# Attention on one core: the value products of a set of scores, issued two sets later and between the halves of a set

## The chip, the core and the metric

The kernel runs on one core of a Trainium2 chip. Its time is the device time of one execution, in microseconds (us); the number to beat or miss is the median of three runs of the kernel before, 2207.93 us (2204.1 to 2208.98). A profile of one execution stands beside it: it was taken in an execution of its own, and that execution has its own time.

The core has engines that run their own instruction streams in order and meet through semaphores: TensorE (PE, with its weight loads shown apart as PEld), VectorE (DVE), ScalarE (ACT), GpSimd (POOL), and SyncE (SP), which issues most of the DMAs.

## The reference, cut to what matters

The block is an attention layer, a mixture of experts, a small mixing layer and the same mixture of experts again, each added to its input. Only the attention is touched. There are 2 sequences of 2048 tokens with 256 features, 16 heads of 16 features, a causal mask, and everything is in float32:

```python
qkv = sn_dense(batch, W_qkv, u_qkv, sigma_qkv)          # x @ (sigma_param / sigma * W)
q, k, v = split_heads(q), split_heads(k), split_heads(v)
att = jnp.einsum('bhqd,bhkd->bhqk', q, k) * scale
att = jnp.where(causal[None, None] == 0, big_neg, att)
att = jax.nn.softmax(att, axis=-1)
x = jnp.einsum('bhqk,bhkd->bhqd', att, v)
x = sn_dense(x, W_proj, u_proj, sigma_proj)
```

## The kernel before

**Tiling.** A *unit* is one sequence b, one chunk c of 512 queries and one group g of 4 heads: 2 x 4 x 4 = 32 units. Each unit has as many *sets* as there are blocks of 128 keys up to its chunk: 4, 8, 12 or 16, 320 in all. The last 4 blocks of keys lie on the diagonal, where a set works on 512, 384, 256 and 128 columns; all other sets have 512. A unit takes its diagonal sets first (`softmaxes`).

**Two passes over the scores.** The row maxima must be known before the exponentials. So the scores are computed twice: once to find the maxima (`Maxima.step`, tiles `psm`, line 341; VectorE reduces each tile, lines 350 and 355), and once more transposed, with the maximum folded in through an extra row of q (`softmaxes`, tiles `st`, line 386; ScalarE takes the exponential into `pt`, line 390; GpSimd blanks the part above the diagonal, line 393). The maxima run some units ahead of the exponentials, and one loop walks both: in one turn of the loop it issues one set of the one and one set of the other.

**One turn of the loop.** A set has two halves of two heads each. In each half come two score products (`st`) and then two products for the maxima (`psm`) on the other half of the array's rows. These products use 32 rows each, so four of them run side by side. Behind the two halves come the *value products* of the set before (`values`, tile `o`, line 405): four products of 128 rows and 32 columns. ScalarE copies `o` out (line 414, or 411 for the first set of a unit), and GpSimd adds it to the accumulator `oa` (line 416). The variable `behind` holds the one set whose value products are still to come.

**What else goes into a turn.** Behind the value products come, in turns that are fixed by a plan: the projection to q and k of a later unit (`prepare`: two transposes `flip`, line 129, then `psk`, line 275, which ScalarE copies out twice, to `qT` and `sk`, lines 285 and 287), the values of a chunk (`make_v`, `psv`, line 301), the end of a unit (`finish`, `pso`, line 423, which VectorE reads, lines 426 and 429), and the output projection of a chunk (`project`: `psf`, line 444, copied by ScalarE; `psj`, line 454, read by VectorE). `after(k, ...)` puts such work at the end of a later turn; this text calls it *side work*.

**What sets the order.** Program order is the order of each engine. All accumulators named above except `st` come from one pool of 4 banks (`ps_m`, function `bank`), handed out round robin: a product may only start when the tile that had its bank four requests earlier has been read out. `st` has two tiles of its own (`ps_st`), `pt` six buffers.

Of the kernel before, what the change touches and what calls it, by code (L numbers as in the profile page):

```python
# [51 lines left out]
def hybrid_block(  # L52
# [87 lines left out]
    with tc.tile_pool(name="aw", bufs=1) as aw, ExitStack() as aw_ctx:  # L140
# [106 lines left out]
        with ExitStack() as ac:  # L247
# [16 lines left out]
            def bank(nm):  # L264
                return ps_m.tile([P, CH], F32, tag="mm", name=nm)
# [135 lines left out]
            def values(b, c, g, n, kb, off, pts):  # L401

                o = bank(f"o_{b}_{g}_{c}_{kb}")
                for j in range(4):
                    nc.tensor.matmul(  # L405
                        o[32 * j:32 * j + 32, off:], V[kb // NB][:, kb % NB, 4 * g + j, :],
                        pts[j // 2][:, j % 2, off:], start=True, stop=True,
                    )
                if n == 0:
                    acc[b, c, g] = oap.tile([P, CH], F32, tag="oa", name=f"oa_{b}_{g}_{c}")  # L410
                    nc.scalar.copy(acc[b, c, g], o)
                else:
                    t = oap.tile([P, CH], F32, tag="op", name=f"op_{b}_{g}_{c}_{kb}", bufs=2)
                    nc.scalar.copy(t[:, off:], o[:, off:])  # L414
                    a = acc[b, c, g]
                    nc.gpsimd.tensor_tensor(a[:, off:], a[:, off:], t[:, off:], ALU.add)  # L416
# [80 lines left out]
            def make_vs(b, c):  # L497

                todo = [(b, c, 0), (b, c, 2)] if (b, c) != LAST else []
                if b == LAST[0] and c == order[b][0]:  # L500
                    todo += [(*LAST, 0), (*LAST, 2)]
                for k, v in enumerate(todo):
                    after(k + 1, make_v, *v)

            tick = [0]
            due = []
# [1 line left out]
            def after(k, fn, *args):  # L508
                due.append((tick[0] + k, fn, args))
# [8 lines left out]
            def count(c):  # L518
                return NB * (c + 1)

            ready, mx, sm, behind = {}, None, None, None
            nm, na = 0, 0
            def scaled(f):
                factors["k"] = f
# [21 lines left out]
            while na < len(units) or due or behind:  # L546
                cols, n_m = CH, CH
                run_a = na < len(units) and ready.get(na, tick[0] + 1) <= tick[0]
                run_m = nm < len(units) and nm - na < QTS - 1 - (nm < EARLY)
                if run_a:  # L550
                    u = units[na]
                    if sm is None:
                        sm = softmaxes(*u)
                        left_a = count(u[1])
                        if u[2] == 0 and u[0] == 1:
                            make_vs(u[0], u[1])
                    done = count(u[1]) - left_a
                    cols = CH - done * P if done < NB else CH
                if run_m:
                    w = units[nm]  # L560
                    if mx is None:
# [4 lines left out]
                        mx = Maxima(*w)  # L566
# [6 lines left out]
                    kc, i = mx.pick(cols)  # L573
                    n_m = (i + 1) * P if kc == w[1] else CH
                for h in range(2):
                    if run_a:
                        got = next(sm)
                    if run_m:
                        mx.step(kc, i, 2 - 2 * h)
                if behind:  # L580
                    values(*behind)
                    behind = None
                if run_a:
                    behind = (*u, *got)
                    left_a -= 1
                    if not left_a:
                        sm, na = None, na + 1
                        after(4, finish, *u)
                        if u[2] == NG - 1:
                            box = {}  # L590
                            for k, i in enumerate((0, 2, 0, 2)):
                                after(5 + k, project, u[0], u[1], i, box)
                if run_m:
                    small_set = n_m <= 256 or not run_a
                    if steps and (small_set or steps == 3 or mx.left <= steps + 1):
# [8 lines left out]
                    if not mx.left:  # L604
                        shift(*w, mx.part, nmax[nm % 2])
                        ready[nm] = tick[0] + LAG
                        mx, nm = None, nm + 1
# [702 lines left out]
```

## Time and profile before

| | |
|---|---|
| median of 3 runs | 2207.93 us (2204.1 to 2208.98) |
| the profiled execution, its own time | 2117.58 us |
| its span, first to last instruction | 2115.8 us |
| mean granted TensorE clock in it | 0.983 |
| attention: first maxima products to last value products | 27.6 to 1139.7 us |
| PE busy over the span | 2010.0 us (95%) |
| DVE busy | 1386.0 us (66%) |
| ACT busy | 1075.5 us (51%) |
| POOL busy | 870.5 us (41%) |

The attention takes a little over half of the span; the experts and the mixing layer follow. "PE busy" counts a stretch in which any product is under way as busy, so gaps of part of the array don't show in it. The start times of the products in the timeline tell more than the share. In the trace each float32 product is two instructions, which are called its two passes in this text: the 4 value products of a set are 8 rows, the 8 products of its two halves are 16.

### The profile page before, as it was taken

Reading aid. Unit: us, or ns where it says so; the run is one execution under the profiler, and the core shown is the slowest. Engines: PE = TensorE matmul, PEld = TensorE weight load, DVE = VectorE, ACT = ScalarE, POOL = GpSimd, SP = SyncE. Lnnn points to the kernel's source line nnn. Section 1 sums busy time; section 2 is a strip of 40 time slices with the busy share of each in tenths; the row PEclk is TensorE's granted clock in tenths of the full one; section 3 lists DMA queues with packets and bytes.
Section 4 is the critical chain, followed back from the end, with each engine's and each line's share of the span. In section 5 each row is a group of like instructions: output and inputs, shape, how many; then the busy total and the mean of one; then the engine's idle time right before and its main releaser. Section 6 shows DMA issues by size and latency. Waiting matters only on the chain.

```text
span 2115.8 us, 36162 instructions
## 1 busy us (share of the span) xinstructions
PE 2010.0 (95%) x11840; PEld 1087.9 (51%) x11840; DVE 1386.0 (66%) x3428; ACT 1075.5 (51%) x1566; POOL 870.5 (41%) x1153
## 2 busy tenths in 40 slices
PE   6999999999999999999998999999999999999993
PEld 3444444444445444444444666655656556655662
DVE  4777777787776777777851546446776378663643
ACT  1657577577776667767784122324433244431330
POOL 4334345254343343434454171605422753346305
PEclk8999999999999999999999999999999999999997
DMA  3212110000000000000002321423210332013523
GB/s 97 77 36 64 34 33 5 10 1 7 6 7 6 6 1 7 4 4 4 2 2 86 135 90 46 150 80 113 80 41 18 130 112 78 28 40 134 165 76 121
DMA packets 87604, 113.04 MB, mean 53 GB/s; under 512 B 16385, under 2 KB 75137, under 8 KB 87297
## 3 DMA queue, kind: packets, MB, share of 16 engines
q1 hardware_dynamic: 73488, 75.08, 11.1%
q0 software_dynamic: 12288, 33.57, 4.8%
q8 instruction: 101, 1.65, 0.3%
q10 hardware_dynamic: 1648, 2.10, 0.3%
q14 instruction: 79, 0.64, 0.1%
HBM read 54.59 MB, written 51.64 MB: 50 GB/s over the span
## 4 chain that ended last, share of the span: by engine, by line
PE 82%; DVE 7%; ACT 3%; issue 3%; POOL 3%; DMA 2%; DVEq 0%; SPq 0%; POOLq 0%; ACTq 0%
PE st L386 15%; PE o L405 13%; PE psm L341 13%; PE eu L1085 10%; PE s L1011 7%; PE ed L1109 5%; PE sy L1028 4%; PE psk L275 3%; PE tr L1070 3%; PE psz L961 1%; PE psj L454 1%; POOL xs L893 1%; PE psv L301 1%; DVE junk L350 1%; PE psl L761 1%
## 5 line engine op out<-in xcount | busy, mean ns | idle before, releaser
L390 ACT ACTIVATE pt<-st 128x1024 f32<-128x1024 f32 (+3 forms) x640 | 556.0, 895 | 176.1 <-PE psm L341 123.3
L341 PE MATMUL psm<-kT,qT 32*128 32x512 f32 (+3 forms) x2560 | 621.8, 565 | 10.7 <-DMA kT<-sk 4.4
L386 PE MATMUL st<-qT,kT 32*128 32x512 f32 (+3 forms) x2560 | 604.8, 553 | 1.3 <-ACT pt L390 1.3
L355 DVE TENSOR_REDUCE part<-psm 128x1 f32<-128x512 f32 x768 | 477.1, 681 | 117.1 <-PE psm L341 113.6
L416 POOL TENSOR_TENSOR oa<-oa,op 128x512 f32<-128x512 f32 (+3 forms) x288 | 313.8, 1090 | 450.5 <-ACT op L414 450.0
L386 PEld LDWEIGHTS st<-qT,kT 32*128 32x128 f32 x2560 | 264.4, 184 | 228.0 <-ACT pt L390 140.5
L341 PEld LDWEIGHTS psm<-kT,qT 32*128 32x128 f32 x2560 | 274.6, 184 | 76.0 <-issue 20.1
L350 DVE CUSTOM_DVE_ANT_0 junk<-psm,maskq 128x384 bf16<-128x384 f32 (+3 forms) x512 | 250.8, 490 | 94.8 <-PE psm L341 29.9
L405 PE MATMUL o<-pt,v 128*32 128x512 f32 (+3 forms) x2560 | 301.2, 541 | 11.2 <-DVE part L355 6.7
L1085 PE MATMUL eu<-we,turned 128*128 x560 | 263.7, 593 | 0.0
L1092 ACT ACTIVATE es<-ea 128x256 f32<-128x256 f32 x156 | 65.0, 417 | 353.9 <-DVE ea L1090 353.8
L1011 PE MATMUL s<-xT_f,ws 128*128 128x512 f32 x512 | 232.6, 598 | 0.0
L920 POOL DMA_INDIRECT yg<-ys,slot x128 | 128.2, 1001 | 233.2 <-issue 84.6
L414 ACT COPY op<-o 128x512 f32<-128x512 f32 (+3 forms) x288 | 148.6, 516 | 64.5 <-PE o L405 46.9
L1090 DVE TENSOR_TENSOR ea<-eu,be 128x512 f32<-128x512 f32 x156 | 107.4, 689 | 109.5 <-PE eu L1085 108.9
L1109 PE MATMUL ed<-we,turned 128*128 x624 | 162.7, 383 | 14.5 <-ACT turned L1075 14.5
L393 POOL TENSOR_SCALAR_AFFINE_SELECT pt<-pt 128x256 f32<-128x256 f32 x256 | 103.0, 409 | 176.9 <-ACT pt L390 173.0
L405 PEld LDWEIGHTS o<-pt,v 128*32 128x32 f32 x2560 | 52.2, 108 | 214.4 <-DVE part L355 124.4
L1109 PEld LDWEIGHTS ed<-we,turned 128*128 128x128 f32 x624 | 116.1, 190 | 88.0 <-issue 49.0
L893 POOL DMA_INDIRECT xs<-xn_f,slot x128 | 124.9, 975 | 86.3 <-DVE slot L847 59.3
L1011 PEld LDWEIGHTS s<-xT_f,ws 128*128 128x128 f32 x512 | 95.3, 192 | 102.7 <-issue 96.4
L1085 PEld LDWEIGHTS eu<-we,turned 128*128 128x128 f32 x560 | 97.6, 190 | 75.1 <-issue 72.9
(268 smaller groups left out, 2099.4 us busy)
## 6 DMA issues: line engine op xcount, KB each, us to landing
xs<-xs SPq DMA_DIRECT2D x156, 128.0 KB
ys<-ey SPq DMA_DIRECT2D x156, 128.0 KB
xs<-zeros SPq DMA_DIRECT2D x78, 128.0 KB
we<-in_we_dram SPq DMA_DIRECT2D x8, 768.0 KB
kT<-sk SPq DMA_DIRECT2D x128, 32.0 KB
out_dram<-x SPq DMA_DIRECT2D x8, 512.0 KB
x<-in_x_dram SPq DMA_DIRECT2D x6, 512.0 KB
be<-in_be_dram SPq DMA_DIRECT2D x1, 3072.0 KB
```

The lines of the kernel that those rows point to most:

```text
L341: nc.tensor.matmul(ps[:, :n], self.q[r, i * P:(i + 1) * P], kT[b, g, kc][r, :n], start=True, stop=True,)
L350: nc.vector.tensor_tensor_reduce(junk[:, :n], ps[:, :n], maskq[:, CH - n:], 1.0, LOW, ALU.add, ALU.max, m,)
L355: nc.vector.reduce_max(m, ps[:, :n], axis=AX.X)
L386: nc.tensor.matmul(st[:, i, off:], k[r, ks], q[r, off:], start=True, stop=True)
L390: nc.scalar.activation(pt[:, :, off:], st[:, :, off:], AF.Exp)
L405: nc.tensor.matmul(o[32 * j:32 * j + 32, off:], V[kb // NB][:, kb % NB, 4 * g + j, :], pts[j // 2][:, j % 2, off:], start=True, stop=True,)
L414: nc.scalar.copy(t[:, off:], o[:, off:])
L416: nc.gpsimd.tensor_tensor(a[:, off:], a[:, off:], t[:, off:], ALU.add)
L893: ins = nc.gpsimd.indirect_dma_start(out=XS[b], out_offset=bass.IndirectOffsetOnAxis(ap=slots[f, b][:, k, n:n + 1], axis=0), in_=xhat[f, b ...
L1011: nc.tensor.matmul(ps, w[:, d, cs], xT[:, d, :], start=d == 0, stop=d == 1)
L1085: nc.tensor.matmul(ps, t[:, 1, d * P:(d + 1) * P], we_s[:, bass.ds(v + d * CH, CH)], start=d == 0, stop=d == 1,)
L1109: nc.tensor.matmul(ps[:, 0:D], t[:, 0, d * P:(d + 1) * P], we_s[:, bass.ds(v + 2 * CH + d * D, D)], start=d == 0, stop=d == 1,)
```

## The change

The value products of a set are issued two turns later instead of one, and between the first and the second half of that turn instead of behind both. For this `behind` becomes a list. When no score set is left to issue, one entry per turn is taken all the same. The end of a unit, the output projection and the values of the second sequence move back by one turn with it. Nothing else changes: no product, copy or DMA is added or removed.

```diff
@@ make_vs
-                    after(k + 1, make_v, *v)
+                    after(k + 2, make_v, *v)
@@
-            ready, mx, sm, behind = {}, None, None, None
+            ready, mx, sm, behind = {}, None, None, []
@@ one turn of the loop
                 for h in range(2):
                     if run_a:
                         got = next(sm)
                     if run_m:
                         mx.step(kc, i, 2 - 2 * h)
-                if behind:
-                    values(*behind)
-                    behind = None
+                    if not h and len(behind) > run_a:
+
+                        values(*behind.pop(0))
                 if run_a:
-                    behind = (*u, *got)
+                    behind.append((*u, *got))
                     left_a -= 1
                     if not left_a:
                         sm, na = None, na + 1
-                        after(4, finish, *u)
+                        after(5, finish, *u)
                         if u[2] == NG - 1:
                             box = {}
                             for k, i in enumerate((0, 2, 0, 2)):
-                                after(5 + k, project, u[0], u[1], i, box)
+                                after(6 + k, project, u[0], u[1], i, box)
```

## The prediction, made before the changed kernel was run

> **What bounds the kernel now.** I read the page first (busy shares, then the chain that ended last), then the waits of the weight loads inside the attention, then the timeline of PE over a few turns. From the page:
>
> ```profile
> PE 2010.0 (95%) x11840; PEld 1087.9 (51%) x11840; DVE 1386.0 (66%) x3428; ACT 1075.5 (51%) x1566; POOL 870.5 (41%) x1153
> PE 82%; DVE 7%; ACT 3%; issue 3%; POOL 3%; DMA 2%; DVEq 0%; SPq 0%; POOLq 0%; ACTq 0%
> PE st L386 15%; PE o L405 13%; PE psm L341 13%; PE eu L1085 10%; PE s L1011 7%; PE ed L1109 5%; PE sy L1028 4%; PE psk L275 3%; PE tr L1070 3%; PE psz L961 1%; PE psj L454 1%; POOL xs L893 1%; PE psv L301 1%; DVE junk L350 1%; PE psl L761 1%
> ```
>
> TensorE carries 82% of the chain, and the three kinds of product of the attention are 41% of it. So time is won or lost by what lies between PE's products. The timeline of PE over one plain turn (start, duration, engine, line, operation, tile, shape, count):
>
> ```profile
> 536.60 0.70 PE L386 MATMUL st<-qT,kT 32*128 32x512 f32 x2
> 537.13 0.59 PE L386 MATMUL st<-qT,kT 32*128 32x512 f32 x2
> 537.57 0.59 PE L386 MATMUL st<-qT,kT 32*128 32x512 f32 x2
> 538.00 0.59 PE L386 MATMUL st<-qT,kT 32*128 32x512 f32 x2
> 538.56 1.06 PE L405 MATMUL o<-pt,v 128*32 128x512 f32 x8
> 539.55 0.70 PE L386 MATMUL st<-qT,kT 32*128 32x512 f32 x2
> ```
>
> Look at the differences of the starts. Inside the scores a pass costs 0.43 us. The first pass behind another kind of product costs 0.53, and from the last pass to the value products it is 0.56. The value products take 0.99 until the scores go on. So a turn is 1.96 + 0.99 = 2.95 us, of which 1.96 - 4 x 0.43 = 0.24 us is the price of entering and leaving the 32-row products. The next turn takes 3.10 (538.56 to the value products at 541.66): every other turn one `psm` is 0.15 to 0.19 late, because VectorE has not yet read its bank. VectorE needs 2.4 us per turn (4 reductions 0.60 apart) and idles 0.5 to 0.8 between them. PE and VectorE are thus nearly in balance.
>
> A turn with side work is different:
>
> ```profile
> 550.68 1.06 PE L405 MATMUL o<-pt,v 128*32 128x512 f32 x8
> 551.68 1.98 PE L275 MATMUL psk<-xnTa,w_qkv 128*128 128x512 f32 x4
> 553.59 0.70 PE L386 MATMUL st<-qT,kT 32*128 32x512 f32 x2
> 555.02 1.12 PE L341 MATMUL psm<-kT,qT 32*128 32x512 f32 x2
> 556.07 1.06 PE L405 MATMUL o<-pt,v 128*32 128x512 f32 x8
> ```
>
> From `o` to `o` it is 5.39 us, though 2.95 + 1.91 (551.68 to 553.59) = 4.86 would do. The fourth `psm` starts at 555.02, where 554.56 was due. Its bank is that of `psk` (four requests earlier), and ScalarE reads that out only in these rows (the second ends at 554.97):
>
> ```profile
> 553.70 0.69 ACT L285 ACTIVATE qT<-psk,fq 128x512 f32<-128x512 f32 x1 [1.24 <-PE psk L275]
> 554.29 0.68 ACT L287 ACTIVATE sk<-psk,f_qkv 128x512 f32<-128x512 f32 x1
> ```
>
> The same on the diagonal, with 128 columns: the block of scores that starts at 582.75 needs 1.48 us to the value products at 584.23, because `psm` waits for `sk`:
>
> ```profile
> 582.22 0.60 PE L423 MATMUL pso<-ident,oa 128*128 128x128 f32 x4
> 583.74 0.56 PE L341 MATMUL psm<-kT,qT 32*128 32x128 f32 x4 [0.26 <-ACT sk L287]
> 584.23 0.64 PE L405 MATMUL o<-pt,v 128*32 128x256 f32 x8
> ```
>
> Last, what the weight loads waited for between 50 and 1142 us (total us, times, longest):
>
> ```profile
> PEld o L405 <- DVE part L355: 124.4, 154, 3.2
> PEld o L405 <- POOL oa L416: 14.9, 19, 0.9
> PEld psm L341 <- ACT sk L287: 12.1, 27, 1.1
> PEld o L405 <- POOL pt L393: 10.6, 17, 1.2
> PEld psm L341 <- DVE v L306: 5.9, 11, 0.9
> ```
>
> The large first row is mostly no loss: in the plain turn above the load of `o` sits 0.76 us idle while the products before it still stream.
>
> **The change, part by part.** *Plain turns: nothing.* Call the half behind the value products X and the other one Y. Before: o X Y o X Y. After: also o X Y o X Y, only that X is now the second half of one set and Y the first half of the next. The banks, ScalarE's order (exponential, exponential, copy of `o`) and VectorE's order turn with it. So the 2.95/3.10 alternation stays. The cover is complete: the same waits with other names.
>
> *Boundaries between kinds of product: a loss.* Side work stood behind the value products, where PE changed its kind anyway. Now it splits X from Y. I counted in the instruction order of both kernels: unbroken runs of 32-row products go from 335 to 423, runs of side work from 93 to 106, runs of value products stay near 319. A run of scores costs 0.24 extra at 512 columns (above); with 128 columns I take 0.20. A run of side work costs 1.91 - 4 x 0.43 = 0.19. So 88 x 0.22 + 13 x 0.19 = 22 us more on PE, if nothing hides it. Here a rule of the Trainium skill speaks against the change: "TensorEngine Tiling (Array Packing)", Tiling Modes, Key Properties, says that a change of the tiling mode, not of the tile alone, drains TensorE. The trace shows that the price exists and how large it is. By the rule alone the sum ends here: slower by 22. By the rows there is a second term, since the split also moves a wait.
>
> *Bank waits behind side work: a gain.* Before, the requests ran o, K, X1, X2, Y1, Y2: Y2 gets the bank of the side work K, one block of scores behind it. After, they run o, X1, X2, K, Y1, Y2, o, X1: the bank of K goes to the X1 behind the next value products, about 1 us (Y) + 1 us (o) later. ScalarE needs 1.4 us for `qT` and `sk`, so the wait is gone. For `psk` in a plain turn: 4.86 + 0.24 = 5.10 instead of 5.39, a gain of 0.29; about 10 such turns, -3 us.
>
> *The diagonal.* I walked one unit by hand with the rows' numbers (pass 0.43, 0.32, 0.22, 0.11; entering +0.10, leaving +0.1; VectorE per `psm` 0.60, and with the mask 0.71, 0.575, 0.44 for 384, 256, 128 columns; a product is readable 0.67 behind its last pass at 512). From the first diagonal set of the unit (572.23) to the seventh turn's scores (590.86) it takes 18.63 us before. After, with time from that same start: the 384 set starts at 2.94 (before 2.96), 256 at 5.85 (5.67), then `psk` alone at 8.56, 128 at 10.47 (10.52), where the second half waits 0.2 for `sk`, `pso` at 12.3, the next sets at 12.9 and 15.5, then a wait for VectorE of about 0.5, and the point with equal work done at 18.1 to 18.2. So -0.45 per unit, with the extra boundaries already in it. VectorE's idle time shrinks by as much, because X1 and X2 give it something to read while K runs (before it sat 2.39 us idle beside `psk`). This holds for units whose diagonal turns carry `psk`, `pso` or `flip`: 24 of 32, -11 us. My walk is good to some 0.3 us per unit, so 24 x 0.3 = 7 us either way.
>
> *Side work that had no such wait.* `psf`, `psj`, lone `flip` and `psv`: some 54 runs. They are small, or are read out quickly, and lose up to 0.24 each with nothing in return, 13 us at most; on the diagonal VectorE is late anyway and hides about half. I take +6.
>
> *GpSimd.* `o` waited for `pt` behind GpSimd's blanking and its 1.27 us addition (14.9 + 10.6 us of load waits). With two sets of lag they are done long before. Most of these waits lay under running products; comparing starts on PE I find 4 us that delayed products. -4 us. The addition moves between the two blankings on GpSimd's queue, which delays the second by 1.3 us; nothing needs it for another set.
>
> *What else moves.* SP's queue keeps its order (the same `kT` and `qT` DMAs in the same turns). `finish`, `project` and `make_v` go one turn later; they are due by the order of the queue, not by time. `pt` has six buffers for three sets: the exponential of set t reuses the buffer of set t-3, whose value products are issued a turn earlier, so no wait. Only the slack of a whole turn becomes half a turn. Last turns: one drained entry more, below 1 us. I value these at nothing, and at 0 to 5 us lost if the six buffers do bind.
>
> The sum: -3 - 11 + 6 - 4 = -12, from about -25 to +15. I round the likeliest to -10, since the walk left out every wait that I didn't see in the trace. The sum is made against the profiled execution, 2117.6 us; the median is 2207.9, 4% longer, and the trace doesn't show what those runs spend it on. I take the same -10 off the median: 2198. Two tenths of a per cent, about 4.4 us, is what can be told from no change.
>
> **The rivals.** *The boundaries decide.* If the waits behind side work only stood in for VectorE's lateness, they come back at the next bank and the split is paid in full: 22 us minus the 4 of GpSimd, +18 us, 2226. It speaks for it that VectorE is late on each diagonal (0.7 us more than the products need even in turns of 256 columns without side work); against it, that VectorE idles 1.66 and 2.39 us next to side work. The point is 0.22 us: where a turn with side work gets back less than that, the change loses. *The two terms cancel*: the diagonal yields 0.2 us per unit instead of 0.45, the rest stays: -3 - 5 + 8 - 2 = -2, 2206. *It is a rotation and more*: VectorE's shorter idle stretches also end the alternation 2.95/3.10 in the plain turns. There are about 176 of them, 0.075 each, -13 on top of -12: 2183. Against it: by the bank order the same late reduction meets the same kind of product.
>
> **How the numbers follow.** The likeliest case (-5 to -20) gets 0.46, the stronger gain 0.06: faster by over 0.2%: 0.52. Cancelling: 0.17. The boundaries decide, or `pt` binds: 0.31. The likeliest case's own range is 2188 to 2203. The range over all runs from 2183, the strong case, to 2222, most of the way to the rival on the other side, which leaves out about 1 in 10 at each end.
>
> **What would show it.** Right: in a turn with `psk` the fourth `psm` no longer waits for `sk`, and from `o` to `o` it is 5.1 us; the waits of `o` for GpSimd are gone; the plain turns still take 2.95 and 3.10; the last value product of the attention starts some 10 us before 1139.7. Wrong: the turns with side work take 5.4 or more; `psm` or `o` has a new row of waits, for `part` or `pt`; the plain turns change.

## The result, and the profile after

The change makes the kernel slower: 2216.61 us median (2209.39 to 2219.16, 18 runs) against 2206.57 us for the kernel before on the same chip (2200.97 to 2209.0, 18 runs). The ratio is 1.0044, with a 95% interval of 1.0036 to 1.0052: 10 us lost where 10 us gained were forecast. The time lies inside the forecast range of 2183 to 2222 us, but only because that range was wide: the way it moved is the wrong one.

The whole loss is in the attention. GpSimd's first memset for the experts comes at 1147.9 us in the trace of before and at 1157.7 us after. (The spans themselves, 2115.8 and 2214.9 us, are not compared: the profiled execution of before spent 968 us behind that memset, every other trace here 1051 to 1057.)

From the page of the changed kernel, the busy times and the chain that ended last:

```profile
PE 2041.7 (92%) x11840; PEld 1074.0 (48%) x11840; DVE 1389.8 (63%) x3428; ACT 1072.0 (48%) x1566; POOL 866.8 (39%) x1153
PE 81%; DVE 6%; another core or an unknown queue 4%; issue 4%; ACT 3%; DMA 1%; POOL 1%; DVEq 0%; SPq 0%; ACTq 0%; POOLq 0%
```

The picture is the same as before: PE carries four fifths of the chain. The waits of the weight loads between 50 and 1142 us (total us, times, longest):

```profile
PEld o L405 <- DVE part L355: 106.8, 140, 1.5
PEld psm L341 <- DVE part L355: 28.5, 73, 2.9
PEld o L405 <- POOL oa L416: 17.4, 23, 0.8
PEld o L405 <- POOL pt L393: 17.4, 30, 0.8
PEld psm L341 <- ACT sk L287: 4.8, 5, 1.1
```

The wait for `sk`, which the change was expected to remove, fell from 12.1 us in 27 waits to 4.8 in 5. The waits of `o` for GpSimd, which were expected to vanish, rose from 25.5 to 34.8 us. And `psm` waits more for VectorE's `part`: 28.5 us in 73 waits, where the kernel before has

```profile
PEld psm L341 <- DVE part L355: 10.3, 36, 0.8
```

A turn with `psk` on the diagonal, in the timeline of PE of the changed kernel:

```profile
584.62 1.98 PE L275 MATMUL psk<-xnTa,w_qkv 128*128 128x512 f32 x4 [0.24 <-DVE part L350]
586.54 0.38 PE L386 MATMUL st<-qT,kT 32*128 32x128 f32 x2
586.55 0.38 PE L341 MATMUL psm<-kT,qT 32*128 32x128 f32 x2
...
586.97 0.85 PE L405 MATMUL o<-pt,v 128*32 128x384 f32 x8
587.75 0.38 PE L386 MATMUL st<-qT,kT 32*128 32x128 f32 x2
...
588.38 0.66 PE L423 MATMUL pso<-ident,oa 128*128 128x128 f32 x4
```

See two things. The second block of 128 columns (587.75) comes without the 0.26 us wait for `sk` that it had before. And the value products beside the smallest scores have 384 columns (0.85 us), where the kernel before had 256 in that turn (0.64 us), and `pso` stands alone behind its own block instead of behind `psk`. These two side effects of the lag turned out to matter more than the place of the value products.

The seventh turn of the same unit (its first set starts at 575.84), first PE, then the weight loads with their waits:

```profile
594.17 0.60 PE L386 MATMUL st<-qT,kT 32*128 32x512 f32 x1
594.73 0.59 PE L386 MATMUL st<-qT,kT 32*128 32x512 f32 x1
```

```profile
593.77 0.29 PEld L341 LDWEIGHTS psm<-kT,qT 32*128 32x128 f32 x2 [0.27 <-DVE part L350]
597.44 0.18 PEld L341 LDWEIGHTS psm<-kT,qT 32*128 32x128 f32 x1 [0.47 <-DVE part L355]
```

Two score products that elsewhere start together (586.54, x2) start 0.56 us apart, and `psm` waits for VectorE. From its first score product to that of the eighth turn, the seventh takes 3.48 us, where it takes 2.96 in the kernel before (medians over the 8 units of 16 sets).

### The profile page after: what moved, and what is told of

Its sections match the earlier page's. It is cut to its first block, busy times and chain, and to the rows that moved or that the text cites. A ratio compares the mean times of both kernels' runs of the same rounds, so it can differ in the third digit from the quotient of the medians.

```text
span 2214.9 us, 36176 instructions
## 1 busy us (share of the span) xinstructions
PE 2041.7 (92%) x11840; PEld 1074.0 (48%) x11840; DVE 1389.8 (63%) x3428; ACT 1072.0 (48%) x1566; POOL 866.8 (39%) x1153
## 4 chain that ended last, share of the span: by engine, by line
PE 81%; DVE 6%; another core or an unknown queue 4%; issue 4%; ACT 3%; DMA 1%; POOL 1%; DVEq 0%; SPq 0%; ACTq 0%; POOLq 0%
PE st L386 18%; PE o L405 12%; PE psm L341 11%; PE eu L1085 10%; PE s L1011 8%; PE ed L1109 5%; PE sy L1028 4%; PE psk L275 3%; PE tr L1070 2%; PE psj L454 1%; PE psz L961 1%; PE psv L301 1%; DVE junk L350 1%; PE psl L761 1%
## 5 line engine op out<-in xcount | busy, mean ns | idle before, releaser
L341 PE MATMUL psm<-kT,qT 32*128 32x512 f32 (+3 forms) x2560 | 637.7, 569 | 8.5 <-DMA kT<-sk 4.1
L386 PE MATMUL st<-qT,kT 32*128 32x512 f32 (+3 forms) x2560 | 629.2, 560 | 0.7 <-ACT pt L390 0.7
L355 DVE TENSOR_REDUCE part<-psm 128x1 f32<-128x512 f32 x768 | 484.8, 684 | 123.0 <-PE psm L341 115.0
L386 PEld LDWEIGHTS st<-qT,kT 32*128 32x128 f32 x2560 | 254.2, 184 | 278.7 <-ACT pt L390 149.4
L341 PEld LDWEIGHTS psm<-kT,qT 32*128 32x128 f32 x2560 | 264.3, 184 | 70.6 <-DVE part L355 28.5
L1011 PE MATMUL s<-xT_f,ws 128*128 128x512 f32 x512 | 237.8, 608 | 13.4 <-ACT hsh L1013 6.9
L1028 PE MATMUL sy<-ws,hsh 128*128 128x256 f32 x512 | 124.8, 393 | 40.1 <-DVE hsh L1016 23.6
```

The source lines that it names most:

```text
L341: nc.tensor.matmul(ps[:, :n], self.q[r, i * P:(i + 1) * P], kT[b, g, kc][r, :n], start=True, stop=True,)
L355: nc.vector.reduce_max(m, ps[:, :n], axis=AX.X)
L386: nc.tensor.matmul(st[:, i, off:], k[r, ks], q[r, off:], start=True, stop=True)
L1011: nc.tensor.matmul(ps, w[:, d, cs], xT[:, d, :], start=d == 0, stop=d == 1)
L1028: nc.tensor.matmul(ps[:, k, :], h[d][:, i * P:(i + 1) * P], ws2_s[:, d, :], start=d == 0, stop=d == 3,)
```

## A view by sets, which depends less on two single executions

A table of turns tells more than two spans. It takes the start of the first exponential of each set from the traces, subtracts that of the set before it, and sets the result against the kernel before; the number is the median over the 8 units of 16 sets. "Set k" is the time from set k to set k+1; sets 0 to 3 are the diagonal with 512, 384, 256 and 128 columns.

| us against the base | set 0 | 1 | 2 | 3 | 4 | 5 | 6 | sum of all 16 |
|---|---|---|---|---|---|---|---|---|
| the change | +0.21 | -0.03 | +0.18 | +0.14 | +0.46 | -0.88 | +0.03 | +0.13 |
| lag alone (e1) | 0.00 | -0.10 | +0.29 | +0.43 | +0.27 | -0.91 | +0.49 | +0.39 |
| lag, unit's end as before, not in the last four units (e13) | 0.00 | -0.10 | +0.31 | +0.21 | +0.27 | -0.91 | +0.49 | +0.21 |
| lag of two up to the plain sets only (e8) | 0.00 | -0.89 | +1.10 | +0.21 | +0.27 | +0.02 | +0.07 | +0.78 |
| none in the last diagonal turn (e16) | 0.00 | 0.00 | 0.00 | -0.77 | +0.42 | +0.02 | 0.00 | -0.33 |
| lag, all 512 wide (e12, base e11) | 0.00 | -0.10 | +0.09 | 0.00 | +0.05 | +0.01 | -0.07 | -0.01 |

The sets from 7 on add up to less than 0.1 us in each row. So the plain turns don't change, as forecast; everything happens on the diagonal and in the two or three turns behind it.

The table leaves out the shorter units. From the first exponential of each unit to that of the next, summed over the 28 units ahead of the last four, but without the 11th and the 20th (each holds a stretch of slow products in one of the two traces, see the end), the change takes 5.8 us more than the kernel before: 0.2 us per unit in the median. The last four units take 3.5 us more (below). Together that is 9.3 of the 9.8 us between the two memsets. The same sum over 26 units is +7.4 us for e13, +4.9 for e14, +11.4 for e8 and -5.1 for e16.

## The experiments

All ratios are to the kernel before on the same chip, with 95% intervals. Boundaries are changes between 32-row products, value products and side work in PE's instruction order: 747 before, 848 in the change.

### First round: lag, place, boundaries, tail

**The lag without the new place (e1), 759 boundaries.**

```diff
-                    if not h and len(behind) > run_a:
-                        values(*behind.pop(0))
+                if len(behind) > run_a:
+                    values(*behind.pop(0))
```

> The lag of two sets alone: the value products stay behind both halves of a turn. Changes of kind on PE, counted in the instruction order: 759 (before 747, with the change 848). Theory A (the split of the scores by side work is paid in full, and what is saved at the bank of the side work comes back as a later wait for VectorE): about the time before, 2203 to 2208, since nearly no boundary is added. Theory B (the second set of lag costs the time: pt has six buffers, and exponentials wait for value products): as slow as the change or slower, 2214 or more.

Measured: 2209.56 us, where the kernel before took 2199.47 on this chip; ratio 1.0047 (1.0034 to 1.006). The lag alone costs as much as the whole change, with 89 boundaries fewer. What the forecast called a rotation that moves nothing is the loss.

**The new place without the lag (e2), 825 boundaries.**

```diff
+                    if not h and behind:
+                        values(*behind)
+                        behind = None
-                if behind:
-                    values(*behind)
-                    behind = None
```

> The place between the halves alone, with a lag of one set as before. 825 changes of kind. The value products now follow the exponential of the half just before them by half a turn less, so they should wait for it: in a plain turn the exponential of the second half ends some 0.2 us after the value products are due (4.18 against 3.96 in the walk of the prediction), 320 turns. Theory A and B both: slower than the change, 2216 plus 30 to 80, because of that wait, which shows as a wait of o for pt. If it is no slower than the change, the second set of lag was not needed.

Measured: 2271.78 us, ratio 1.0329 (1.0315 to 1.0342). The place between the halves needs the second set of lag: the median turn without side work takes 3.23 us from `o` to `o` instead of 2.96, over 236 turns some 64 of the 72 us. In the trace the value products at 545.86 take 1.73 us instead of 1.06; the exponential of their second half ends at 546.70.

**The change with its side work held back to the value products (e3), 747 boundaries.**

```diff
                 for _, fn, args in now:
-                    fn(*args)
+                    side.append((fn, args))
...
@@ behind the value products, between the halves
+                        while side:
+                            f, args = side.pop(0)
+                            f(*args)
```

> The change, with the side work (q and k projection, values, ends of units, output projection, statistics) held back to directly behind the next value products, so that o, K, X, Y stand as before; the lag of two stays. 747 changes of kind, exactly as before. Theory A: the loss is gone, 2201 to 2208, as before or up to 5 less for the waits on GpSimd that are gone. Theory B (lag or tail): it stays at 2213 or more.

Measured: 2215.5 us, ratio 1.0068 (1.0055 to 1.0082). A hundred boundaries fewer than the change (the steps of `prepare` and of the statistics are held back too), and no faster: by the ratios slower. So the rival "the boundaries decide" isn't what happened.

**The change with the old place in turns without maxima (e4).**

```diff
-                    if not h and len(behind) > run_a:
+                    if h != run_m and len(behind) > run_a:
```

> The change, but in turns without maxima (the last 20 or so of the attention, and few others) the value products stand behind both halves again, still two sets late. Theory A says nothing of these turns. Theory C (the last turns lose some 3.5 us of the 10, because two halves that ran side by side on PE are now pulled apart by the value products while ScalarE waits for them): 2211 to 2214. If C is wrong: 2215 to 2218 as the change.

Measured: 2210.66 us, ratio 1.0051 (1.0038 to 1.0064): no gain. The place in the last turns isn't it either.

### Second round: is it VectorE?

A new theory, D: the lag moves the *widths*. The value products of the four diagonal sets have 512, 384, 256 and 128 columns. With a lag of one they follow the sets 1, 2, 3 and 4, with a lag of two the sets 2, 3, 4 and 5. Two views show why that might matter. The first is VectorE's timeline behind the diagonal in the kernel before:

```profile
585.03 0.08 DVE L350 DVE_READ_ACCUMULATOR2_ANT part<- 128x1 f32 x1
586.02 2.48 DVE L355 TENSOR_REDUCE part<-psm 128x1 f32<-128x512 f32 x4 [0.90 <-PE psm L341]
588.52 0.69 DVE L350 CUSTOM_DVE_ANT_0 junk<-psm,maskq 128x512 bf16<-128x512 f32 x1
...
589.36 0.69 DVE L350 CUSTOM_DVE_ANT_0 junk<-psm,maskq 128x512 bf16<-128x512 f32 x1
...
591.78 0.19 DVE L359 TENSOR_REDUCE nmax<-part 128x16 f32<-128x32 f32 x1
592.00 0.31 DVE L363 STREAM_TRANSPOSE nmt<-nmax 128x128 f32<-128x128 f32 x1
592.24 2.45 DVE L355 TENSOR_REDUCE part<-psm 128x1 f32<-128x512 f32 x4
```

The second is the same stretch of the same unit with the lag alone:

```profile
591.33 2.48 DVE L355 TENSOR_REDUCE part<-psm 128x1 f32<-128x512 f32 x4 [0.39 <-PE psm L341]
593.96 0.69 DVE L350 CUSTOM_DVE_ANT_0 junk<-psm,maskq 128x512 bf16<-128x512 f32 x1
...
597.22 0.18 DVE L359 TENSOR_REDUCE nmax<-part 128x16 f32<-128x32 f32 x1
597.44 0.31 DVE L363 STREAM_TRANSPOSE nmt<-nmax 128x128 f32<-128x128 f32 x1
597.67 1.25 DVE L355 TENSOR_REDUCE part<-psm 128x1 f32<-128x512 f32 x2
```

Behind the first long reduction of each stretch no row is marked with idle time before it (the view marks pauses of more than 0.15 us): VectorE works without a pause. Its four masked reductions of 512 columns are 0.84 us apart instead of 0.60, and the end of the maxima follows. From the first reduction of the stretch to the first one behind `nmt` it takes 6.22 us before (586.02 to 592.24) and 6.34 us with the lag (591.33 to 597.67), although PE has 256 columns of value products less to do in it. So PE's work seems to be largely free here, and the lag moved work out of it.

**Half reductions, to take VectorE out (e5 before, e6 lag alone, e7 the change).** The same edit in three kernels; only the first half of the columns enters the maximum:

```diff
-                                junk[:, :n], ps[:, :n], maskq[:, CH - n:], 1.0, LOW,
+                                junk[:, :n // 2], ps[:, :n // 2], maskq[:, CH - n:CH - n // 2], 1.0, LOW,
...
-                            nc.vector.reduce_max(m, ps[:, :n], axis=AX.X)
+                            nc.vector.reduce_max(m, ps[:, :n // 2], axis=AX.X)
```

> The kernel before, in which VectorE's reductions for the row maxima read only the first half of the columns of each tile (the other half of the keys is left out of the maximum; the products are all made). One reduction takes about 0.35 us instead of 0.60, the masked one of 512 columns about 0.45 instead of 0.84, so VectorE is no longer near its bound anywhere in the attention. This is the base for the next two runs. Theory D (with a lag of two sets the wide value products of the diagonal, 256 columns more per unit, move ahead of the stretch behind the diagonal in which VectorE is the bound, so their time is paid and not given back) and its rivals agree here: faster than the kernel before by 15 to 60 us, since the 0.15 us of every other plain turn and the waits behind the diagonal go.

> The lag of two sets alone (value products behind both halves, as before), with the same half reductions. Theory D: without a stretch bound by VectorE it doesn't matter where the widths stand, so the gap to the before with half reductions is within 3 us, where it was 10 with whole reductions. Rival P (the lag itself costs: six pt buffers for three sets, or GpSimd's order of additions and blankings): the gap stays at 7 us or more.

> The whole change with the same half reductions. Nothing is hidden behind VectorE any more, so this shows the price of the 101 additional boundaries by itself, less the waits behind side work that it takes away. Theory D: some 88 x 0.22 + 13 x 0.19 = 22 us less 4 to 12, so 10 to 18 us slower than the before with half reductions, and nearly all of that beyond the lag alone with half reductions. Rival P: as with whole reductions, 7 to 11 us, and no more than the lag alone.

Measured: 2138.04, 2146.57 and 2144.49 us; ratios 0.9722, 0.976 and 0.9749 (each within 0.0014). The base is 62 us faster, a little more than the 15 to 60 that were expected. The gap of the lag is still 8.5 us where D asked for under 3, and the change is not 10 to 18 but 6.5 us slower. D fell as it was put: something else in the lag costs, which VectorE doesn't hide. And the change, with 89 boundaries more, isn't slower than the lag alone even here; what they cost and what the split gains aren't separated by it.

**A lag of two up to the first plain set, drained behind it (e8).**

```diff
-                if behind:
-                    values(*behind)
-                    behind = None
+                keep = run_a and u[1] > 0 and 1 <= got[0] <= NB
+                while len(behind) > keep:
+                    values(*behind.pop(0))
```

> The kernel before (lag of one set, value products behind both halves), but in units with more than 4 sets the turn of the second diagonal set issues no value products; the lag is then two sets up to the first plain set, and the second plain turn issues two sets of value products (128 and 512 columns). So 256 columns of value products less per unit stand ahead of the stretch behind the diagonal, and more in it. Theory D: 0.24 to 0.5 us less per unit in 28 units, 4 to 12 us faster than the kernel before. Rival P (a lag of two on the diagonal costs by itself, through pt or GpSimd): 3 to 10 us slower.

Measured: 2212.36 us, ratio 1.0058 (1.0044 to 1.0072): 12 us slower, where D asked for 4 to 12 faster and the rival for 3 to 10 slower. (As in e1, `behind` is a list.) The table says why. The turn of set 1 has no value products, 0.99 us less, and set 1 is 0.89 shorter; but set 2 gives 1.10 back at once, of which only 0.24 are its own wider value products. VectorE's timeline there, in this kernel:

```profile
581.88 0.56 DVE L350 CUSTOM_DVE_ANT_0 junk<-psm,maskq 128x384 bf16<-128x384 f32 x1 [0.26 <-PE psm L341]
...
583.30 0.56 DVE L350 CUSTOM_DVE_ANT_0 junk<-psm,maskq 128x384 bf16<-128x384 f32 x1
583.78 0.08 DVE L350 DVE_READ_ACCUMULATOR2_ANT part<- 128x1 f32 x1
584.01 0.56 DVE L350 CUSTOM_DVE_ANT_0 junk<-psm,maskq 128x384 bf16<-128x384 f32 x1
584.49 0.08 DVE L350 DVE_READ_ACCUMULATOR2_ANT part<- 128x1 f32 x1
584.72 0.42 DVE L350 CUSTOM_DVE_ANT_0 junk<-psm,maskq 128x256 bf16<-128x256 f32 x1
...
586.80 0.08 DVE L350 DVE_READ_ACCUMULATOR2_ANT part<- 128x1 f32 x1
```

The same reductions in the kernel before, the first and the last row:

```profile
576.20 0.56 DVE L350 CUSTOM_DVE_ANT_0 junk<-psm,maskq 128x384 bf16<-128x384 f32 x1 [0.26 <-PE psm L341]
...
581.12 0.08 DVE L350 DVE_READ_ACCUMULATOR2_ANT part<- 128x1 f32 x1
```

So there is a second stretch without a pause: the masked reductions of 384 columns, 0.71 us apart, and those of 256. From the first of them to the end of the last it takes 5.00 us in both kernels (581.88 to 586.88 here, 576.20 to 581.20 before). The value products of 512 columns that stood in that turn had been free. Taken out of it they bought nothing, while the wider ones in the turns of sets 3 and 4 were paid (+0.21, +0.27). By these rows D had the right mechanism and the wrong map: the free places are the turns of set 1 and set 5, the paid ones those of sets 2, 3 and 4. (With the lag alone, set 5 gives 0.91 us back for its 384 columns less, but set 6 takes 0.49 of that: half free.)

### Third round: the two places of the loss

A lag of two puts 512, 384 and 256 columns into the three paid turns, in place of 384, 256 and 128. And the unit's end (`finish`, `project`) stands one turn later, so `pso` no longer shares a run with `psk`. Theory E names these two and the last four units.

**The lag, but not in the last four units (e10, the edit against e1).**

```diff
-                if len(behind) > run_a:
+                keep = run_a and na < len(units) - NG
+                while len(behind) > keep:
```

> The lag of two sets alone (value products behind both halves), but the last four units, in which no maxima are left to compute, keep a lag of one. In the profiles those four units and what follows them take 45.1 us in the kernel before and 48.2 with the lag, with the clock in its slow windows counted. Theory E (the loss has three places: 3 us in the last four units, 2 to 3 us for the end of a unit that stands one turn later in a run of its own, and 3 to 5 us for the wide value products that move from turns in which VectorE is late into turns in which PE is): 3 us faster than the lag alone, so ratio about 1.003 to the kernel before. Rival P (a lag of two sets costs at every set, by its buffers): no more than 0.5 us faster than the lag alone, ratio 1.0045 to 1.0055.

Measured: 2217.01 us with 2205.61 before, ratio 1.0048 (1.0033 to 1.0063), as its rival had it. No gain over the lag alone (1.0047): this part of E fell.

**As e10, and the unit's end in its old turns (e13), 739 boundaries.**

```diff
-                        after(5, finish, *u)
+                        after(4, finish, *u)
...
-                                after(6 + k, project, u[0], u[1], i, box)
+                                after(5 + k, project, u[0], u[1], i, box)
```

> As the run before, and the end of a unit and the output projection stand in the turns in which the kernel before has them, so that the transposes of a unit's end share a run with the projection to q and k; 739 boundaries between kinds of product instead of 756 (the kernel before has 747). Theory E: another 17 x 0.2 = 3 us less, ratio 1.001 to 1.002 to the kernel before; what is then left is the widths. Rival P: no change against the run before.

Measured: 2211.53 us on the same chip, ratio 1.003 (1.0019 to 1.0041), where 1.001 to 1.002 was forecast: 5.5 us less than e10 by the medians, though the intervals overlap. In the table, set 3's +0.43 becomes +0.21 in this kernel. The last four units lose too. From their first exponential to the first `psf` of the last projection it takes

| before | the change | e1 | e10 | e13 | e14 |
|---|---|---|---|---|---|
| 38.3 us | 41.8 | 41.4 | 40.1 | 39.6 | 40.2 |

These times come back from trace to trace where the last units are alike: 38.3 us in e5, e8, e17 and e19, which end as the kernel before does, and 41.9 in e7, which ends as the change does. The 41.4 of e1 have a stretch of slow products in them; e6, which ends alike, takes 39.9.

**All value products 512 wide (e11 before, e12 as e13).** The same addition in both, behind the four products of a set:

```diff
+                for at in range(0, off, CH - off):
+                    to = min(at + CH - off, off)
+                    for j in range(4):
+                        nc.tensor.matmul(
+                            o[32 * j:32 * j + 32, at:to], V[kb // NB][:, kb % NB, 4 * g + j, :],
+                            pts[j // 2][:, j % 2, off:off + to - at], start=True, stop=True,
+                        )
```

> The kernel before, in which the value products of the diagonal sets are made 512 columns wide by extra products into columns of the same tile that nothing reads (128, 256 and 384 columns more). It is the base for the next run: every turn then has value products of the same width, so it doesn't matter by how many sets they lag. All theories: 768 columns more per unit at 0.24 us per 128 are 1.4 us, 46 us over 32 units, of which what lies in turns bound by VectorE is hidden: 25 to 46 us slower than the kernel before.

> The lag of two sets with the last four units and the side work as in the kernel before (as the second run), and all value products 512 columns wide. Theory E: no width is left to move, so the gap to the before with 512 columns everywhere is within 2 us either way. Rival P: the gap stays at 6 to 10 us.

Measured: 2230.11 and 2232.35 us, ratios 1.0109 (1.0092 to 1.0126) and 1.0116 (1.0099 to 1.0134). The base is 24.5 us slower than the kernel before (25 to 46 were expected). With nothing left to move, the gap of 6 us is down to 2, within what these runs can tell from nothing. With four runs each the medians alone hardly separate 2 us from 6. The traces do: the last row of the table shows each turn alike to 0.1 us, and over the 26 units e12 takes 1.6 us less than e11, where e13 takes 7.4 more than the kernel before. The widths are the second place.

### Fourth round: the place by itself, and the other direction

**The change with the unit's end and the last four units as before (e14, 808 boundaries), and the same with all 512 wide (e15).**

```diff
-                    if not h and len(behind) > run_a:
-
+                    if near and not h and len(behind) > run_a:
                         values(*behind.pop(0))
+                while behind and not near:
+                    values(*behind.pop(0))
...
-                        after(5, finish, *u)
+                        after(4, finish, *u)
```

Here `near` is `na < len(units) - NG`; `project` moves as in e13, and e15 adds the products of e11.

> The whole change (lag of two sets, between the halves), but the end of a unit and the output projection stand in the turns of the kernel before, and the last four units have the lag and the place of before; 808 boundaries instead of 848. Theory E (the loss is in the later turn of the unit's end and in the widths; the place between the halves costs its boundaries and gains as much from the bank waits): 3 to 5 us faster than the change, ratio 1.002 to 1.003, equal to the lag alone with the same two corrections (1.003). Theory B (the boundaries decide): 69 more of them than in that run are 10 to 15 us, ratio 1.007 or more. Theory W (the place between the halves is a gain by itself): below 1.001.

> As the run before, and all value products of the diagonal 512 columns wide by extra products that nothing reads, so that no width is moved; to be set against the kernel before and the lag with the same 512 columns (1.0109 and 1.0116). Theory E: within 3 us of both, ratio 1.010 to 1.013. Theory B: 10 to 15 us slower, 1.016 or more. Theory W: 5 us or more faster, below 1.009.

Measured: 2211.82 us, ratio 1.0022 (1.0014 to 1.0029), half of the change's loss; and 2231.95 us, ratio 1.0118 (1.0099 to 1.0136), equal to both kernels with 512 columns everywhere. The place between the halves, once the widths and the unit's end are out of the way, neither costs nor gives anything that these runs show: 69 boundaries more than e13, and the same time within the intervals.

**No value products in the turn of the last diagonal set (e16), 709 boundaries.** The kernel before with

```diff
-                if behind:
-                    values(*behind)
-                    behind = None
+                keep = run_a and u[1] > 0 and got[0] in (NB - 1, NB)
+                while len(behind) > keep:
+                    values(*behind.pop(0))
```

> The kernel before with a lag of one, but in units of more than 4 sets the turn of the last diagonal set (128 columns) issues no value products; the next turn issues 256 columns instead of 128, and the one after it 128 and 512. The widths move from turns bound by PE into the stretch behind the diagonal in which VectorE is late, and there is one run of value products less per unit (709 boundaries instead of 747). Theory E: 0.2 to 0.5 us less in each of 28 units, 6 to 14 us faster, ratio 0.994 to 0.997. Rival L (the last diagonal turn waits for ScalarE's copies anyway, so nothing is won there, and the wider product of the next turn is paid, 0.27 us as in the run that drained behind the diagonal): 1.001 to 1.004.

Measured: 2200.63 us, where the kernel before took 2206.79 (37 runs); ratio 0.9972 (0.9965 to 0.998). Faster than both kernels. VectorE's timeline at the same place as above, in this kernel:

```profile
582.04 0.29 DVE L350 CUSTOM_DVE_ANT_0 junk<-psm,maskq 128x128 bf16<-128x128 f32 x1
582.25 0.08 DVE L350 DVE_READ_ACCUMULATOR2_ANT part<- 128x1 f32 x1
582.47 2.48 DVE L355 TENSOR_REDUCE part<-psm 128x1 f32<-128x512 f32 x4
```

The 0.90 us that VectorE stood idle before its 2.48 us are gone, since the scores behind the last diagonal set no longer queue behind 0.57 us of value products on PE. Set 3 gets 0.77 us shorter, set 4 pays 0.42 for its wider value products, and the 640 columns in the turn of set 5 are free (+0.02). The size is at the low edge of the forecast: 6.2 us from the medians where 6 to 14 was put, and a ratio of 0.9972 where 0.994 to 0.997 was.

**Value products for two sets at once in every second plain turn (e17), 611 boundaries.** As e16, with

```diff
+                keep = run_a and got[0] > NB + 1 and got[0] % 2 == 0
```

> The kernel before, but in plain turns (from the third one behind the diagonal) only every second turn issues value products, for two sets at once; 611 boundaries instead of 747. If each boundary is worth 0.22 us there: 72 runs of value products less give up to 16 us, ratio 0.993 to 0.997. Rival V (a turn without value products asks 2.4 us of VectorE in 1.96 us of PE, so PE waits for VectorE what the boundary gave): 0.999 to 1.005.

Measured: 2238.75 us, ratio 1.015 (1.0132 to 1.0169). 136 boundaries fewer, 32 us slower, and outside of both forecasts (0.993 to 0.997, or 0.999 to 1.005). Two plain turns get 0.65 us shorter and then 1.25 longer. The timeline of PE in the turn behind one without value products:

```profile
549.34 0.59 PE L386 MATMUL st<-qT,kT 32*128 32x512 f32 x2
550.18 0.70 PE L386 MATMUL st<-qT,kT 32*128 32x512 f32 x2 [0.25 <-ACT pt L390]
...
552.22 0.59 PE L341 MATMUL psm<-kT,qT 32*128 32x512 f32 x1
552.74 1.92 PE L405 MATMUL o<-pt,v 128*32 128x512 f32 x16
```

PE has nothing to fill the time with: the scores wait for ScalarE's exponential, and from 550.18 to the value products it takes 2.56 us for a block of 1.96. **The same with half reductions (e19), and the lag of e13 with half reductions (e18):**

> Value products of two sets at once in every second plain turn, with reductions that read half of the columns, so that VectorE is late nowhere; to be set against the kernel before with half reductions (ratio 0.9722). If VectorE alone ate the gain of the 136 boundaries: 10 to 17 us faster than that, ratio 0.964 to 0.968. If ScalarE does too (two exponentials of 1.02 us and a copy of 0.59 in a turn, and score products have two tiles only): the score products of a turn without value products wait for the exponentials, and the gain is gone, 0.971 to 0.980.

> The lag of two sets with the unit's end, the output projection and the last four units as in the kernel before, and with reductions that read half of the columns; to be set against the kernel before with half reductions (2138.0 us, ratio 0.9722) and the lag alone with them (2146.6, 0.976). Theory E: the widths cost little where PE is the bound in every turn, and the later unit's end was the rest, so within 3 us of the before with half reductions, ratio 0.971 to 0.9736. Rival P (something else in the lag costs): 0.975 or more.

Measured: 2160.52 us, ratio 0.9793 (0.9779 to 0.9806), so 0.7% slower than e5. With VectorE out of the way the pairs still lose, so VectorE alone is not the reason: the forecast for the case that ScalarE holds them back is met, though no run takes ScalarE away. And 2146.99 us, ratio 0.9732 (0.9719 to 0.9745), within 2.2 us of e5's 0.9722, on another chip. By the ratios, most of what e6 had left open is in what e18 puts back: the unit's end and the last four units.

## Why the prediction was wrong, point by point

- **"Plain turns: nothing."** Right: the median from `o` to `o` in turns without side work is 2.96 us before and after, and the sets from 7 on don't move. What failed is the step from plain turns to the whole: a rotation is free only where all sets are alike, and on the diagonal they are 512, 384, 256 and 128 wide.
- **"Boundaries between kinds of product": 22 us if nothing hides it.** It can stand as an upper bound, and the second term that was set against it exists. Their sum is zero within what these runs can tell (e14 against e13, e15 against e11 and e12). The Trainium skill's rule about a change of the tiling mode in "TensorEngine Tiling (Array Packing)", Tiling Modes, Key Properties, is not contradicted: the timeline shows a price (0.24 us for a run of scores, 0.19 for one of side work, as worked out in the prediction), but in this kernel the count of boundaries predicted no result. e3 and e17 have fewer and are slower. The rival at 2226 had the way right, and its cause isn't the one that was found.
- **"Bank waits behind side work: a gain."** Right in kind and size: the waits for `sk` fell from 27 to 5, and the plain turns with `psk` alone that took 5.39 us from `o` to `o` take 5.04 to 5.09; the forecast was 5.10. The lag alone leaves them at 5.39 (e1), so the place gives this. In return `st` waits for `qT` and `sk`, 10.0 us in 15 waits, each under value products that still run. Only the number of such turns was off: three, not about 10, so -1.0 us instead of -3.
- **"The diagonal": -0.45 us per unit, -11 us in all.** The step that failed, in its term for VectorE ("then a wait for VectorE of about 0.5"). Up to the seventh turn the walk was good: there the first score product comes 18.33 us after the unit's start (18.1 to 18.2 forecast, 18.63 before), and in the median over the units of 16 sets 18.17 against 18.63. But by then VectorE's lateness was not yet paid for. The second product comes only at 18.89, and the seventh turn takes 3.48 us instead of 2.96. At the first score product of the eighth turn nothing is left of the gain (medians of 21.65 us in both kernels), and over all sets the sum is +0.13. VectorE's lateness, which the walk put at 0.5 us once, belongs to a stretch of some 6 us without a pause. The narrower value products there returned less than the wider ones ahead of it had cost.
- **"`finish`, `project` and `make_v` go one turn later": valued at nothing.** Wrong: some 5 us by the medians (e14 against the change, together with the lag and the place in the last four units; e13 against e10). That they aren't urgent was the wrong question. Their place decides whether `pso` shares a run with `psk`; that this is the way it costs is argued, not shown by itself.
- **"Side work that had no such wait": +6.** Not measured by itself; e14 and e15 say only that all costs and gains of the place cancel.
- **"GpSimd": -4 us.** Wrong in kind: the load waits of `o` for `pt` and `oa` didn't go but rose from 25.5 to 34.8 us. How much of either held up a product was not measured.
- **"Last turns: below 1 us."** Wrong: 38.3 us became 41.8 (first exponential of the last four units to the last projection's first `psf`).
- **"0 to 5 us lost if the six buffers do bind."** No run tried more buffers. With equal widths and the unit's end in its turn the lag of two costs about 2 us by the medians and nothing in the traces of the 26 units (e12 against e11), so little room is left for them.

The loss of 10 us thus comes from the lag. The medians give some 5 us to the later end of a unit together with the last four units, and what is left (5 us in e14, 6 in e13) goes when the widths are equal, with the place between the halves at about nothing. The traces place nearly all of it: 3.5 us in the last four units and 5.8 in the 26 units compared above. How the loss divides between the two causes is known only to a few us.

## What to carry to other kernels

A change that delays one stage by a whole number of iterations is neutral only where the iterations are alike: where shapes vary, list which shape lands beside which partner, and mark for each turn which engine works without a pause. Here PE's value products were free beside such a stretch of VectorE (the turns of sets 1 and 5) and paid for in the turns between, so moving wide pieces into one such turn gave 0.28%, with five lines, where moving all pieces by the same step lost 0.44%. Work that "isn't urgent" still has a neighbour that it shares a mode change with: count it before calling its move free.

## What the runs showed of the hardware that was not expected

PE runs at half clock for short stretches. The granted clock in stretches of the changed kernel's trace (window, us, busy time and instructions of PE, PEld, DVE, ACT and POOL, then the clock, DMA share and GB/s):

```profile
355.00:360.00 5.00, 5.00 (x24) 1.07 (x20) 1.98 (x3) 1.61 (x2) 5.00 (x5) 0.50 0.00 0
360.00:364.00 4.00, 4.00 (x28) 0.93 (x20) 2.44 (x4) 2.05 (x2) 1.39 (x3) 0.59 0.00 0
364.00:367.40 3.40, 3.22 (x35) 1.37 (x33) 2.22 (x6) 2.60 (x4) 2.39 (x4) 1.00 0.00 0
```

In the timeline, a pass of the scores that costs 0.43 us elsewhere costs 0.87 there (359.98 to 360.85):

```profile
359.98 1.06 PE L386 MATMUL st<-qT,kT 32*128 32x512 f32 x2
359.99 1.90 PE L341 MATMUL psm<-kT,qT 32*128 32x512 f32 x4
360.85 1.06 PE L386 MATMUL st<-qT,kT 32*128 32x512 f32 x2
```

The kernel before has such a stretch at another place (clock 0.78 on average from 735 to 741 us). The unit that holds it takes 3.6 us longer there than in the change, and the 11th unit, which holds the stretch shown, takes 4.8 us longer in the change: some 4 us each, nearly half of what the change is worth. That is why the readings above rest on medians and leave these units out.

Most of these stretches follow PE's longest pauses, in which it waits for VectorE. The first row is the product behind such a pause in the change, already slow (1.22 us where 0.70 is usual); the second is that of the kernel before, whose products slow down from 730.64 on:

```profile
353.39 1.22 PE L341 MATMUL psm<-kT,qT 32*128 32x512 f32 x1 [2.06 <-DVE part L355]
729.00 0.43 PE L405 MATMUL o<-pt,v 128*32 128x128 f32 x8 [1.75 <-DVE part L355]
```

Over all traces, between 60 us and the last four units, 16 of 22 stretches at half clock begin within 4 us of the end of a pause of PE of 1.4 to 2.4 us. The pause alone isn't enough: in the kernel before the longest one has only products of usual length behind it.

```profile
353.04 1.06 PE L405 MATMUL o<-pt,v 128*32 128x512 f32 x8 [2.35 <-DVE part L355]
```

What else decides is not shown here.

And half of the columns don't take half of VectorE's time: the reductions of 256 columns come 0.34 us apart in e5, those of 512 columns 0.60 us apart.
